# The first stage of a sparse graph kernel: other buffers, another order of row work and searches, weights loaded at its end

## The chip, the cores and the metric

The kernel runs on one core of one Trainium2 chip. The metric is the device time of one execution in microseconds. Over three runs it was 2909.53 (median; 2902.95 to 2912.19).

## What is computed

The input is a batch of 8 feature matrices x (2048 nodes by 128 features) and one adjacency matrix (2048 by 2048, 0 or 1, on average 16 ones in a row). Four graph layers follow each other:

```python
# layers 0 and 1: attention over the neighbours, 8 heads
scores = where(adj == 0, -inf, Q @ K.T / 4);  attn_out = softmax(scores) @ V
x = layer_norm(h + attn_out @ Wo + bo);  x = layer_norm(x + relu(x @ W1 + b1) @ W2 + b2)
# layers 2 and 3: graph attention
e = leaky_relu(s_i + s_j), -inf where adj == 0
x = layer_norm(softmax(e) @ (x @ W) + x)
```

## The kernel before, in words

Because the matrix is sparse, `sparse_path` (L90) never forms the 2048 by 2048 scores. For each node it makes a list of neighbours, and in each layer it gathers the neighbours' rows from a table in DRAM (keys and values of all 8 batches, 8 KB a node in layers 0 and 1). Nodes are sorted by their number of neighbours, so that 16 blocks of 128 nodes have lists of nearly equal length. A block is 128 nodes everywhere below, t counts blocks.

`start()` (L934) is the first stage. It does three things for each of 16 blocks:

- **Search.** `neighbours(t)` (L1019), on DVE: one masking pass over 128 rows of adjacency (L1022: column number where the entry isn't 0), then 16 maximum searches over segments of 128 columns (L1028), which leave 128 candidates a node. `load_adj` (L959) brings the 1 MB of adjacency over SP's queue into one of six buffers; the load for t+6 is issued when the mask of t is done. POOL stores the candidates to `found` (L1030). ACT counts the empty candidates (L1031, into `none`) and, in an iteration later, sums the kept ones (`rest`).
- **Count.** `count(t)` (L1038), on POOL for the first 15 blocks and on DVE for the last: from `none` it makes two 64-column masks, which PE adds into `places` in PSUM (L1001). After the last block, `places` gives every node its rank.
- **Rows.** `turn_x(t)` (L970): PE transposes 8 tiles of x, two ACT copies take them from PSUM, and ACT issues the load of x for block t+4. `first_rows(t)` (L978): 16 products with the key and value weights of layer 0 (L539), four ACT copies (L545) into one of two 1 MB buffers `tops`, and an ACT-issued store to the table in DRAM (L985). Block t uses the buffer of block t-2.

The loop (L1068) runs search t, count t-1, rest t-1, turning of block t-1 and rows of block t-2, in this order; each engine has its own in-order queue, so the order of these calls is the order on every engine. After the loop come the last count, turning of block 15, rows of block 14, the ranks (L1084 to L1121, which end in `perm`, the sorted order), the rows of block 15, the list of neighbours of the first block (`find_lists(0)`, L366), two DVE memsets (L1129, L1130), and `fetch()` (L1131), which issues the first ten gathers on POOL (L321). Then the rank column is copied to DRAM (L1132) and the zero rows of two tables are written (L1135).

The weights, 19 small loads in the list `waiting`, are issued on SP after the first six adjacency loads (L1064). `prepare()` (L256) readies them as a generator that is advanced at t = 4 and t = 6 of the loop, and run to its end in `layers()` (L1269): it centres columns and rows on DVE, multiplies small vectors on PE (L266, L279) into the PSUM tile `pair`, and adds the results on DVE.

The seven large buffers `bufs` hold all of this in the first stage (x in 0, turned x in 1, `tops` in 2, adjacency in 3 to 5, masks and candidates in 6) and the gathered rows afterwards, so parts that were never written are set to zero (L942, L1074, L1129, L1130).

A DMA is issued by SP, ACT or POOL. Those of SP and ACT take eight completion semaphores in turn; the compiled program lists for each DMA which earlier one its issuing engine waits for.

Of the kernel before, what the change touches and what calls it, by code (L numbers as in the profile page):

```python
# [9 lines left out]
F32 = mybir.dt.float32  # L10
# [3 lines left out]
I32 = mybir.dt.int32  # L14
AF = mybir.ActivationFunctionType
# [3 lines left out]
P = 128  # L19
# [14 lines left out]
RING = 9  # L34
STATES = 4
SCALED = 1

# [15 lines left out]
BINS = 64  # L53
# [36 lines left out]
def sparse_path(ctx: ExitStack, tc: tile.TileContext, ins: dict, out: bass.AP, flag: bass.AP):  # L90
# [157 lines left out]
    def centered(w):  # L248

        m = small.tile([P, 1], F32, tag="mean", name="mean")  # L250
        m = m[: w.shape[0], :]
        nc.vector.tensor_reduce(m, w, axis=AX.X, op=ALU.add)
        nc.vector.tensor_scalar_mul(m, m, -1.0 / D)
        nc.vector.tensor_scalar_add(w, w, m)

    def prepare():  # L256

        for l in (0, 1):
            w = W[l]
# [4 lines left out]
            pb = pair  # L264
            for f in range(2):
                nc.tensor.matmul(  # L266
                    pb[:, f : f + 1], w["1"][:, f * P : (f + 1) * P], w["col"][:, 6:7],
                    start=f == 0, stop=f == 1, skip_group_check=True,
                )
            yield  # L270
            nc.vector.tensor_sub(w["col"][:, 4:6], w["col"][:, 4:6], pb[:, :2])
            nc.vector.tensor_add(w["col"][:, 1:2], w["col"][:, 1:2], w["col"][:, 6:7])
            for f in range(2):
                centered(w["2"][:, f, :])
            yield
        for l in (2, 3):
            w = W[l]
            pa = pair
            nc.tensor.matmul(pa[:, :2], w["T"], w["col"][:, 2:4], start=True, stop=True)  # L279
            yield  # L280
            nc.vector.tensor_copy(w["h"][:, D : D + 2], pa[:, :2])
            centered(w["h"][:, :D])

    def width(l):
        return NB * (2 * D if l < 2 else D + 2)
# [246 lines left out]
    def project(l, i, xT, rows, t):  # L532

        w = W[l]
        wide = 2 * D if l < 2 else D + 2
        for h in range(i, i + 4, 2):
            pp = misc()[:, : 2 * wide].rearrange("p (b c) -> p b c", c=wide)
            for j in range(2):
                nc.tensor.matmul(  # L539
                    pp[:, j, :], xT[:, h + j, :], w["qkv"][:, D:] if l < 2 else w["h"],  # L540
                    start=j == 0, stop=True, skip_group_check=True,
                )
            yield
            if l < 2:
                nc.scalar.copy(  # L545
                    rows[:, h * wide : (h + 2) * wide], pp.rearrange("p b c -> p (b c)")
                )
# [386 lines left out]
    def start():  # L934


        adj = [bufs[3 + i // 2][:, i % 2 * N : (i % 2 + 1) * N].bitcast(I32) for i in range(6)]
        xs = [bufs[0][:, i * B * D : (i + 1) * B * D] for i in range(4)]
        xTs = [bufs[1][:, i * B * D : (i + 1) * B * D] for i in range(4)]
        tops = [bufs[2][:, i * width(0) : (i + 1) * width(0)] for i in range(2)]  # L940
        for i in range(3):
            nc.vector.memset(bufs[i][:, 2 * N :], 0.0)  # L942
        cands = bufs[6][:, NT * BINS : NT * BINS + NT * P].rearrange("p (t s c) -> p t s c", t=NT, c=8)
        falling = small.tile([P, BINS], F16, tag="falling", name="falling", bufs=1)
# [13 lines left out]

        def load_adj(t):  # L959
            if t < NT:  # L960
                nc.sync.dma_start(adj[t % 6], ins["adj"][t * P : (t + 1) * P, :])

        def load_x(t):
            if t < NT:
# [13 lines left out]
        def first_rows(t):  # L978
            if t < 0:
                return  # L980
            xT = turned(t)
            for i in range(0, B, 4):
                for _ in project(0, i, xT, tops[t % 2], t):
                    pass
            nc.scalar.dma_start(tables[0][t * P : (t + 1) * P, :], tops[t % 2])  # L985

# [32 lines left out]
        def neighbours(t):  # L1019
            val = work.tile([P, NB, D], F32, tag="q", name="val")  # L1020
            val = val.rearrange("p s c -> p (s c)").bitcast(F16)[:, :N]
            nc.vector.scalar_tensor_tensor(  # L1022
                val, adj[t % 6], 0.0, iota1, op0=ALU.not_equal, op1=ALU.mult,
                accum_out=every_sum[:, t : t + 1],
            )
            load_adj(t + 6)
            for i in range(N // SEG):
                nc.vector.max(cands[:, t, i, :], val[:, i * SEG : (i + 1) * SEG])  # L1028
# [9 lines left out]
        def count(t):  # L1038

            eng = nc.gpsimd if t + 1 < NT else nc.vector  # L1040
            d = small.tile([P, 1], F32, tag="d", name="d")
            eng.tensor_scalar_max(d, none[:, t : t + 1], float(N // SEG * 8 - BINS + 1))
# [24 lines left out]
        rest = None  # L1067
        for t in range(NT):  # L1068
            now_rest = neighbours(t)
            if t > 0:  # L1070
                count(t - 1)
                rest()
            if t in (11, 13):
                nc.gpsimd.memset(bufs[{11: 5, 13: 3}[t]], 0.0)  # L1074
            rest = now_rest
            turn_x(t - 1)
            first_rows(t - 2)
            if t in (4, 6):
                next(weights, None)
        count(NT - 1)  # L1080
        turn_x(NT - 1)
        first_rows(NT - 2)

        picked = bufs[0][:, : NT * BINS].rearrange("p (t c) -> p t c", c=BINS)  # L1084
        nc.vector.tensor_mul(picked, places, same)
        rank = small.tile([P, NT], F32, tag="rank", name="rank", bufs=1)
        nc.vector.tensor_reduce(rank, picked, axis=AX.X, op=ALU.add)
# [1 line left out]
        nc.vector.tensor_single_scalar(largest, rank, float(P), op=ALU.is_lt)  # L1089


        up = bufs[0][:, N : N + NT * (NT + 1)].rearrange("p (t h) -> p t h", h=NT + 1)
# [8 lines left out]
        high = bufs[0][:, N + 512 : N + 512 + NT * NT].rearrange("p (t h) -> p t h", h=NT)  # L1101
# [19 lines left out]
        nc.vector.tensor_add(perm, part1, pn[:, NT : 2 * NT])  # L1121
# [7 lines left out]
        nc.vector.memset(bufs[4], 0.0)  # L1129
# [731 lines left out]
```

## Time and profile before

| what | value |
|---|---|
| median of three runs | 2909.53 us |
| profiled execution | 2798.62 us |
| its span | 2796.7 us, granted TensorE clock 0.939 |
| busy, share of the span | PE 84%, DVE 90%, ACT 49%, POOL 63% |
| DMA | 973.64 MB, mean 348 GB/s |
| adjacency loads, 16 of 1024 KB | 15.6 us from issue to landing (median) |
| table stores of the first stage, 16 of 1024 KB | 4.5 us |
| x loads, 16 of 512 KB | 9.9 us |

The first stage by stretches of the profiled execution:

| us from the start | PE busy | DVE busy | ACT busy | DMA, GB/s |
|---|---|---|---|---|
| 20 to 30 | 6.14 of 10 | 9.97 | 3.13 | 312 |
| 60 to 80 | 13.34 of 20 | 19.86 | 7.78 | 423 |
| 98 to 116 | 16.46 of 18 | 0.52 | 13.70 | 258 |
| 116 to 131 | 13.01 of 15 | 9.49 | 11.47 | 151 |
| 131 to 152 | 13.14 of 21 | 15.44 | 6.29 | 235 |

How to read the profile's rows: a row of a timeline has the start in us, the busy time in us, the engine (with a q: its queue, which issues DMAs or waits), the line of the kernel, the operation, what is written from what, the shapes and the count; in square brackets stand the idle time of the engine before it and what ended that. A row of the view of waits has who waited, for what, the us in total, the times, and the longest. A row of the chain has the start, the duration and what the end of the stage hung on.

### The profile page before, as it was taken

How to read it: one execution, taken by the hardware profiler on the slowest of the kernel's cores; microseconds unless marked ns; L12 is line 12 of the kernel's file. 1: busy time of each engine (PE TensorE's matmuls, PEld its weight loads, DVE VectorE, ACT ScalarE, POOL GpSimd, SP SyncE). 2: the span in 40 equal slices, each digit the busy share in tenths (PEclk: the TensorE clock that was granted, in tenths of full speed). 3: DMA queues.
4: the chain of work that ended last, by engine and by line, in shares of the span. 5: the costliest groups of instructions: out<-in, count | busy, mean ns of one | idle time of the engine just before them, and what ended most of it. 6: DMA issues, size and time to landing. Idle time of an engine off the chain costs nothing.

```text
span 2796.7 us, 48901 instructions
## 1 busy us (share of the span) xinstructions
PE 2345.7 (84%) x17811; PEld 2126.5 (76%) x17811; DVE 2513.7 (90%) x2467; ACT 1381.6 (49%) x5032; POOL 1755.3 (63%) x1346
## 2 busy tenths in 40 slices
PE   5866889898899998798989999997677887878885
PEld 4655788787788887688878888886567776878885
DVE  9698999999899897999999999986889997799995
ACT  3611444454455665154445556566346566355554
POOL 3367788678656454545565566562776776677772
PEclk9978999999999999999999999999789888999997
DMA  9898999999999888789999999984999998999994
GB/s 365 275 373 311 369 349 345 376 338 350 369 337 355 336 320 315 306 320 369 348 390 369 354 374 368 349 328 172 367 412 413 375 367 326 347 411 413 406 402 157
DMA packets 195426, 973.64 MB, mean 348 GB/s; under 512 B 30012, under 2 KB 31804, under 8 KB 123184
## 3 DMA queue, kind: packets, MB, share of 16 engines
q0 software_dynamic: 172080, 885.06, 82.5%
q1 hardware_dynamic: 18346, 60.00, 5.5%
q10 hardware_dynamic: 4752, 25.36, 2.7%
q8 instruction: 144, 2.36, 0.3%
q14 instruction: 104, 0.85, 0.1%
HBM read 917.09 MB, written 87.36 MB: 359 GB/s over the span
## 4 chain that ended last, share of the span: by engine, by line
PE 42%; DVE 24%; DMA 16%; issue 8%; ACT 8%; POOL 1%; ACTq 0%; POOLq 0%; DVEq 0%; SPq 0%
PE acc L335 15%; DMA kv<-table,lists 9%; DVE kv L695 8%; DVE kv L657 8%; PE pair L335 4%; PE m L793 4%; PE m L776 3%; PE m L539 3%; PE m L342 2%; DVE kv L838 2%; PE m L788 2%; PE m L593 2%; PE m L759 2%; PE m L763 2%; DMA table<-rows,perm 2%
## 5 line engine op out<-in xcount | busy, mean ns | idle before, releaser
L321 POOL DMA_INDIRECT kv<-table,lists x938 | 1282.2, 1367 | 678.0 <-PE acc L335 269.8
L335 PE MATMUL acc<-ident,kv 128*128 128x128 f32 x8048 | 1052.9, 285 | 159.6 <-DVE kv L695 87.9
L335 PEld LDWEIGHTS acc<-ident,kv 128*128 128x128 f32 x8048 | 957.6, 148 | 222.4 <-DVE kv L695 111.1
L695 DVE TENSOR_TENSOR kv<-kv,weights 128x2048 f32<-128x2048 f32 (+1 forms) x282 | 625.8, 2219 | 25.9 <-ACT weights L687 25.8
L657 DVE TENSOR_TENSOR kv<-kv,q 128x2048 f32<-128x2048 f32 (+1 forms) x280 | 618.2, 2208 | 32.0 <-DMA kv<-table,lists 26.3
L838 DVE TENSOR_TENSOR kv<-kv,pair 128x3584 f32<-128x3584 f32 (+1 forms) x150 | 530.8, 3538 | 1.0
L335 PE MATMUL pair<-ident,kv 128*128 128x128 f32 (+1 forms) x2256 | 301.3, 277 | 86.1 <-issue 72.8
L663 DVE TENSOR_TENSOR kv<-kv 128x1024 f32<-128x1024 f32 (+1 forms) x282 | 334.8, 1187 | 9.2
L335 PEld LDWEIGHTS pair<-ident,kv 128*128 128x128 f32 (+1 forms) x2256 | 257.0, 141 | 106.4 <-issue 85.1
L321 POOL DMA_INDIRECT kv<-table,sorted_lists x150 | 192.8, 1286 | 139.7 <-PE acc L335 42.9
L679 ACT ACTIVATE ring<-pair 128x128 f32<-128x128 f32 (+1 forms) x282 | 77.8, 276 | 365.0 <-PE pair L335 292.9
L502 ACT ACTIVATE n<-m,eps 128x128 f32<-128x128 f32 x512 | 181.5, 371 | 137.6 <-PE m L793 133.3
L687 ACT COPY weights<-pair 128x128 f32<-128x128 f32 (+1 forms) x282 | 73.3, 260 | 350.9 <-PE pair L683 342.7
L843 ACT ACTIVATE kv<-kv,ws 128x128 f32<-128x128 f32 x544 | 174.5, 398 | 145.0 <-DVE ws L832 136.4
L793 PE MATMUL m<-w_L,hT 128*128 128x128 f32 x1024 | 157.3, 276 | 0.0
L509 ACT ACTIVATE n<-m,rs 128x128 f32<-128x128 f32 x512 | 146.4, 376 | 0.3
L793 PEld LDWEIGHTS m<-w_L,hT 128*128 128x128 f32 x1024 | 136.1, 193 | 0.0
L776 PE MATMUL m<-n1T,w_L 128*128 128x512 f32 x256 | 132.9, 604 | 3.0 <-ACT hT L781 1.8
L723 DVE TENSOR_TENSOR o<-acc,scale 128x512 f32<-128x512 f32 x128 | 83.3, 684 | 52.0 <-ACT scale L741 27.1
L526 POOL DMA_INDIRECT table<-rows,perm x57 | 82.1, 1441 | 70.1 <-ACT own L562 18.7
L342 PE MATMUL m<-ident,n 128*128 128x128 f32 x640 | 114.9, 293 | 11.9 <-ACT n L509 5.6
L342 PEld LDWEIGHTS m<-ident,n 128*128 128x128 f32 x640 | 79.6, 145 | 51.0 <-ACT n L509 23.3
(254 smaller groups left out, 3614.2 us busy)
## 6 DMA issues: line engine op xcount, KB each, us to landing
kept<-xT SPq DMA_DIRECT2D x40, 512.0 KB, 6.7
kv<-in_adj_dram SPq DMA_DIRECT2D x16, 1024.0 KB, 15.6
table<-kv ACTq DMA_DIRECT2D x16, 1024.0 KB, 4.5
xT<-kept SPq DMA_DIRECT2D x32, 512.0 KB, 8.0
kv<-table,lists POOLq DMA_INDIRECT x938, 8.6
kv<-in_x_nodes_dram ACTq DMA_DIRECT2D x16, 512.0 KB, 9.9
kv<-table,sorted_lists POOLq DMA_INDIRECT x150, 6.9
home<-kept SPq DMA_DIRECT2D x4, 512.0 KB, 15.3
```

The costliest lines, as they stand in the source:

```text
L321: this = nc.gpsimd.indirect_dma_start(out=dst, out_offset=None, in_=tables[l][:, :] if need == NT else views[l][0], in_offset=bass.Indirec ...
L335: nc.tensor.matmul(dst, src, ident, start=start, stop=True, is_transpose=True, skip_group_check=True)
L342: nc.tensor.transpose(pt[:, j * P : (j + 1) * P], src[:, j, :], ident)
L502: nc.scalar.activation(dst[:, i, :], z[:, i, :], AF.Square, bias=eps, scale=D**-0.5, accum_out=ss[:, i : i + 1],)
L509: nc.scalar.mul(dst[:, i, :], z[:, i, :], rs[:, i : i + 1])
L657: nc.vector.tensor_mul(kk, kk, q[:, None].to_broadcast([P, ns, NB, D]))
L663: nc.vector.tensor_add(hk.rearrange("p j (c h) -> p c j h", h=NH), kj[:, :, :NH, :], kj[:, :, NH:, :])
L695: nc.vector.tensor_mul(vv, vv, w.rearrange("p (s b h) -> p (s b) h", b=NB, h=NH)[:, :, None, :] .to_broadcast([P, ns * NB, HD, NH]),)
L776: nc.tensor.matmul(ph, wt["1"][:, f * P : (f + 1) * P], n1T.rearrange("p b c -> p (b c)"), start=True, stop=True,)
L793: nc.tensor.matmul(y[:, j, :], hT[:, f, j, :], wt["2"][:, f, :], start=False, stop=f == 1, skip_group_check=True,)
L838: nc.vector.tensor_mul(hv[:, :, :nv, :], hv[:, :, :nv, :], wc[:, :, :nv, None].to_broadcast([P, ns, nv, D]))
L843: nc.scalar.mul(hv[:, i, b, :], hv[:, i, b, :], ws[:, i, b - nv : b - nv + 1])
```

## The change

Four edits, all in `start()`, `prepare()` and the first lines of `layers()`:

- Buffers: four `tops` instead of two, four adjacency buffers instead of six.
- Order in the loop: search t; then, except at t = 5, 8 and 11, turning of the next block and rows of the one before it; then count t-1, rest t-1; then `ended()` with the store of candidates and the count of empty ones. So turning starts with block 0 at t = 0. Thirteen blocks are turned in the loop; block 13 is turned after the last count, 14 after `perm`, 15 after the first list. For the last block DVE counts the empty candidates itself.
- Weights: their 19 loads follow the adjacency loads on SP; the zero rows follow them, then the rank column. `prepare()` has three parts, all run in `layers()`.
- Zeroing: on POOL after `perm`, instead of POOL in the loop and DVE before the first gathers. The rank arithmetic uses buffers 3 and 6 instead of 0.

```diff
+BEHIND = (5, 8, 11)
...
-        adj = [bufs[3 + i // 2][:, i % 2 * N : (i % 2 + 1) * N].bitcast(I32) for i in range(6)]
+        adj = [bufs[3 + i // 2][:, i % 2 * N : (i % 2 + 1) * N].bitcast(I32) for i in range(4)]
...
-        tops = [bufs[2][:, i * width(0) : (i + 1) * width(0)] for i in range(2)]
-        for i in range(3):
+        tops = [bufs[2 + 3 * (i // 2)][:, i % 2 * width(0) : (i % 2 + 1) * width(0)] for i in range(4)]
+        for i in (0, 1, 2, 5):
             nc.vector.memset(bufs[i][:, 2 * N :], 0.0)
...
-            nc.gpsimd.dma_start(found[t * P : (t + 1) * P, :], every)
-            total(every, AF.Relu, none[:, t : t + 1], bias=onesc, scale=-1.0)
-            return lambda: total(every, AF.Copy, kept_sum[:, t : t + 1])
+
+            def ended():
+                nc.gpsimd.dma_start(found[t * P : (t + 1) * P, :], every)
+                if t + 1 < NT:
+                    total(every, AF.Relu, none[:, t : t + 1], bias=onesc, scale=-1.0)
+                    return
+                empty = small.tile([P, P], F32, tag="partial", name="empty")
+                nc.vector.tensor_single_scalar(empty, every, 0.0, op=ALU.is_equal)
+                nc.vector.tensor_reduce(none[:, t : t + 1], empty, axis=AX.X, op=ALU.add)
+
+            return ended, lambda: total(every, AF.Copy, kept_sum[:, t : t + 1])
...
-        for t in range(6):
+        for t in range(4):
             load_adj(t)
-            if t < 4:
-                load_x(t)
-        for dst, src in waiting:
-            nc.sync.dma_start(dst, src)
-
+            load_x(t)
         rest = None
+        turned_so_far = 0
         for t in range(NT):
-            now_rest = neighbours(t)
+            ended, now_rest = neighbours(t)
+            if t not in BEHIND:
+                turn_x(turned_so_far)
+                first_rows(turned_so_far - 1)
+                turned_so_far += 1
             if t > 0:
                 count(t - 1)
                 rest()
-            if t in (11, 13):
-                nc.gpsimd.memset(bufs[{11: 5, 13: 3}[t]], 0.0)
+            ended()
             rest = now_rest
-            turn_x(t - 1)
-            first_rows(t - 2)
-            if t in (4, 6):
-                next(weights, None)
         count(NT - 1)
-        turn_x(NT - 1)
-        first_rows(NT - 2)
+        turn_x(turned_so_far)
+        first_rows(turned_so_far - 1)
...
-        first_rows(NT - 1)
+        nc.gpsimd.memset(bufs[3], 0.0)
+        nc.gpsimd.memset(bufs[4], 0.0)
+        nc.gpsimd.memset(spot, 0.0)
+        turn_x(turned_so_far + 1)
+        first_rows(turned_so_far)
...
-        nc.vector.memset(bufs[4], 0.0)
-        nc.vector.memset(bufs[6][:, NT * (BINS + P) :], 0.0)
+        for t in range(turned_so_far + 2, NT + 1):
+            if t < NT:
+                turn_x(t)
+            first_rows(t - 1)
+        for dst, src in waiting:
+            nc.sync.dma_start(dst, src)
+        for l in (2, 3):
+            nc.sync.dma_start(tables[l][N : N + 1, :], bufs[3][:1, : width(l)])
         fetch()
         nc.sync.dma_start(ranks.rearrange("(t p) o -> p (t o)", p=P), rank)
         rest()
-        for l in (2, 3):
-            nc.sync.dma_start(tables[l][N : N + 1, :], bufs[5][:1, : width(l)])
...
         begin(every[0])
+        next(weights, None)
         drain()
```

`prepare()` after the change: the first part centres the rows and matrices of layers 0 and 1 on DVE, the second runs all small products of the four layers on PE into columns of `pair`, the third adds and copies their results on DVE.

More of the change, by code (lines that the diff above doesn't have):

```diff
@@ L263, in prepare @@
             w["row_z"] = parts(row_z, f"z{l}")
-            pb = pair
+            for f in range(2):
+                centered(w["2"][:, f, :])
+        yield
+        for l in range(4):
+            w = W[l]
+            if l > 1:
+                nc.tensor.matmul(
+                    pair[:, 2 * l : 2 * l + 2], w["T"], w["col"][:, 2:4], start=False, stop=l == 3,
+                    skip_group_check=True,
+                )
+                continue
             for f in range(2):
                 nc.tensor.matmul(
-                    pb[:, f : f + 1], w["1"][:, f * P : (f + 1) * P], w["col"][:, 6:7],
-                    start=f == 0, stop=f == 1, skip_group_check=True,
-                )
-            yield
-            nc.vector.tensor_sub(w["col"][:, 4:6], w["col"][:, 4:6], pb[:, :2])
+                    pair[:, 2 * l + f : 2 * l + f + 1], w["1"][:, f * P : (f + 1) * P],
+                    w["col"][:, 6:7], start=l + f == 0, stop=False, skip_group_check=True,
+                )
+        yield
+        for l in (0, 1):
+            w = W[l]
+            nc.vector.tensor_sub(w["col"][:, 4:6], w["col"][:, 4:6], pair[:, 2 * l : 2 * l + 2])
             nc.vector.tensor_add(w["col"][:, 1:2], w["col"][:, 1:2], w["col"][:, 6:7])
-            for f in range(2):
-                centered(w["2"][:, f, :])
-            yield
         for l in (2, 3):
[L277 to L282, printed above, removed]
+            nc.vector.tensor_copy(W[l]["h"][:, D : D + 2], pair[:, 2 * l : 2 * l + 2])
+            centered(W[l]["h"][:, :D])
     def width(l):
@@ L960, in load_adj @@
             if t < NT:
-                nc.sync.dma_start(adj[t % 6], ins["adj"][t * P : (t + 1) * P, :])
+                nc.sync.dma_start(adj[t % 4], ins["adj"][t * P : (t + 1) * P, :])
         def load_x(t):
@@ L982, in first_rows @@
             for i in range(0, B, 4):
-                for _ in project(0, i, xT, tops[t % 2], t):
+                for _ in project(0, i, xT, tops[t % 4], t):
                     pass
-            nc.scalar.dma_start(tables[0][t * P : (t + 1) * P, :], tops[t % 2])
+            nc.scalar.dma_start(tables[0][t * P : (t + 1) * P, :], tops[t % 4])
         none = small.tile([P, NT], F32, tag="none", name="none", bufs=1)
@@ L1022, in neighbours @@
             nc.vector.scalar_tensor_tensor(
-                val, adj[t % 6], 0.0, iota1, op0=ALU.not_equal, op1=ALU.mult,
+                val, adj[t % 4], 0.0, iota1, op0=ALU.not_equal, op1=ALU.mult,
                 accum_out=every_sum[:, t : t + 1],
             )
-            load_adj(t + 6)
+            load_adj(t + 4)
             for i in range(N // SEG):
@@ L1040, in count @@
             eng = nc.gpsimd if t + 1 < NT else nc.vector
-            d = small.tile([P, 1], F32, tag="d", name="d")
+            d = small.tile([P, 1], F32, tag="d" if t + 1 < NT else "mean", name="d")
             eng.tensor_scalar_max(d, none[:, t : t + 1], float(N // SEG * 8 - BINS + 1))
@@ L1072, in start @@
                 rest()
-            if t in (11, 13):
-                nc.gpsimd.memset(bufs[{11: 5, 13: 3}[t]], 0.0)
+            ended()
             rest = now_rest
-            turn_x(t - 1)
-            first_rows(t - 2)
-            if t in (4, 6):
-                next(weights, None)
         count(NT - 1)
-        turn_x(NT - 1)
-        first_rows(NT - 2)
-        picked = bufs[0][:, : NT * BINS].rearrange("p (t c) -> p t c", c=BINS)
+        turn_x(turned_so_far)
+        first_rows(turned_so_far - 1)
+        picked = bufs[3][:, : NT * BINS].rearrange("p (t c) -> p t c", c=BINS)
         nc.vector.tensor_mul(picked, places, same)
@@ L1089, in start @@
         nc.vector.tensor_single_scalar(largest, rank, float(P), op=ALU.is_lt)
-        up = bufs[0][:, N : N + NT * (NT + 1)].rearrange("p (t h) -> p t h", h=NT + 1)
+        spot = bufs[6][:, NT * (BINS + P) :]
+        up = spot[:, : NT * (NT + 1)].rearrange("p (t h) -> p t h", h=NT + 1)
         nc.vector.tensor_tensor(
@@ L1100, in start @@
         nc.vector.tensor_scalar_add(lo1, lo1, float(P + 1))
-        high = bufs[0][:, N + 512 : N + 512 + NT * NT].rearrange("p (t h) -> p t h", h=NT)
+        high = spot[:, NT * (NT + 1) : NT * (2 * NT + 1)].rearrange("p (t h) -> p t h", h=NT)
         nc.vector.tensor_sub(high, up[:, :, :NT], up[:, :, 1:])
```

## The prediction

> **What bounds the kernel now.** I read the page first: DVE is busy 90% of the span, PE 84%, and nothing in the change touches the four layers, so only the first stage, up to the first gathered rows, is in question. The view of waits, taken over the first 152 us, has one large entry on DVE and one on ACT:
>
> ```profile
> DVE d L1042 <- ACT junk L1017: 17.4, 1, 17.4
> ACT kv L545 <- DMA table<-kv: 19.9, 5, 4.3
> ACT junk L1017 <- DMA w_L<-in_L_w_dram: 3.2, 1, 3.2
> ```
>
> The timeline of DVE gives them a place:
>
> ```profile
> 92.85 2.27 DVE L1022 SCALAR_TENSOR_TENSOR val<-kv,iota 128x2048 f16<-128x2048 int32 x1
> 95.17 3.19 DVE L1028 MAX8 kv<-val 128x8 f32<-128x128 f16 x16
> 115.81 0.15 DVE L1042 TENSOR_SCALAR d<-none 128x1 f32<-128x1 f32 x1 [17.44 <-ACT junk L1017]
> 119.93 1.22 DVE L1085 TENSOR_TENSOR kv<-places,kv 128x1024 f32<-128x1024 f32 x1 [3.55 <-PE places L1001]
> ...
> 130.71 0.17 DVE L1121 TENSOR_TENSOR perm<-part,m 128x16 int32<-128x16 f32 x1
> ...
> 151.75 2.29 DVE L657 TENSOR_TENSOR kv<-kv,q 128x2048 f32<-128x2048 f32 x1 [2.14 <-DMA kv<-table,lists]
> ```
>
> The searches end at 98.36; DVE then stands until ACT has counted the last block's empty places at 115.8, because that count is queued in ACT behind the row work (turning x, projecting, storing a block). The row work goes on to the end of the stage:
>
> ```profile
> 88.84 0.33 ACTq L985 DMA_DIRECT2D table<-kv  x1
> ...
> 124.82 0.33 ACTq L985 DMA_DIRECT2D table<-kv  x1
> 125.19 4.85 ACT L1111 ACTIVATE chosen<-kv,largest 128x128 f16<-128x128 f32 x16 [0.40 <-DVE low L1113]
> ...
> 137.24 0.33 ACTq L985 DMA_DIRECT2D table<-kv  x1
> ```
>
> and the first gather on POOL stands after it:
>
> ```profile
> 142.41 1.02 POOL L321 DMA_INDIRECT kv<-table,lists  x1 [10.15 <-DVE kv L1129]
> ```
>
> A gather may read any row, so it needs all sixteen table stores. 137.24 plus the median landing of a store in the page (4.5) is 141.7; the DVE memset (L1129, ends 141.99) is named as releaser, but takes less than 1 us more. So the stage's end is the sixteenth store. What held the row work back, before it ran at 5.20 us a block (83.64 to 120.03, seven blocks), the chain of the first 160 us shows:
>
> ```profile
> 33.50 11.25 DMA table<-kv
> 44.81 22.41 DMA kv<-in_adj_dram
> 67.30 13.84 DMA table<-kv
> ```
>
> An adjacency load (44.81, landing 67.2) releases the issue of a *table store* (67.30). They share no data. In the compiled program the DMAs that SP and ACT issue take eight completion semaphores in turn, so each waits, in its issuing engine's queue, for an earlier DMA of either engine. The 3.2 us entry above is another such wait: ACT held by a weight load at its x load.
>
> **The change, part by part.** Times are on the profiled execution: 2798.62, of which 2796.7 is the span and 1.9 lies around it. It is 110.9 us (3.8%) under the median of 2909.53; I carry the difference in us over unscaled, since 3.8% of a few us is nothing.
>
> *Searches.* One is 5.43 us (92.85 less 49.42, over eight). Weight preparation leaves DVE's middle: 33.47 to 37.02 and 47.89 to 49.42, 5.1 us. From 6.31 the sixteen end at 93.2 instead of 98.36. With four adjacency buffers the load of t+4 is issued when the mask of t is done; it has 4 x 5.43 - 2.3 = 19.4 us against a median landing of 15.6 (min 5.6, max 23.4, under three or four loads in flight). Here about one is in flight, so I take 7, and no starving of DVE.
>
> *The last count on DVE*: two small operations (near 0.3 each, as L252's 0.27) in place of the 17.4 us wait. What is late next is `places`: PE does the last count's additions after the row work queued before it.
>
> *Row work first, and four table buffers.* PE starts turning x near 8 instead of 20.8, and the 19.9 us of waits for table buffers go. DMA bandwidth can carry it: by the end of the searches 16.8 MB adjacency, 8.4 MB x, 12.6 MB of tables and 0.9 MB found, 38.7 MB. From 60 to 80 us the stretches show 423 GB/s: 91.5 us. The Trainium skill (DMA: Bandwidth & Descriptors, "Where 436 GB/s comes from") says that HBM binds such transfers at about 358 GB/s: 108 us, and the searches would starve. The trace decides; I use 423.
>
> *Weights last: the new wait.* SP issues the 19 weight loads only after adjacency load 15. The compiled order names who waits for whom: table store 6 waits for adjacency load 14; the x load of block 12, issued by ACT in iteration 10, waits for L1's qkv weights, which wait for adjacency load 15; table store 7 waits for L2's column weights, seven issues further on. Load 14 cannot be issued before 6.31 + 10 x 5.43 + 2.3 = 62.9, load 15 not before 68.3. So store 6, due at 60.4, goes at about 70; load 15 lands at 75.3; qkv lands 3.5 later (its row in the page of DMAs) at 78.8, where ACT, freed by store 6 at 70 and through with turning by 72, gets on. Its four row copies take 2.7; L2's columns are issued at 75.3 + 7 x 0.45 = 78.5 and land at 82. Store 7 goes at 82, against 88.84 now. Behind the waiting DMA in ACT stand the copies that empty PSUM (so PE stops), and the counts that POOL and PE wait for.
>
> *From there to the sixteenth store.* Now: 88.84 to 137.24, 48.4. After: to store 8, 5.2 plus 2.6 for the late count of block 10 (ACT 0.7, then POOL's 1.3 + 0.46 + part of 0.44) that PE meets ahead of its next block: 89.8. Three blocks at 5.2: store 11 at 105.4. `places` 1 us later, so DVE's L1085 at 106.5 (13.4 earlier than 119.93), `perm` at 117.5. But three blocks (BEHIND skips three iterations) now come after `perm`: turning 14 (1.5) and projecting 13 as block 15 now (130.36 on PE to 137.24: 6.9): store 13 at 125.4; one turn and block at 6.5, between 5.2 and 8.4 by PE's clock (0.74 in 131 to 152): 131.9; one block without a turn, 4 to 6.9: 137. The sixteenth store is issued at 137.0, against 137.24. What the searches give is spent in the wait for weights and on the blocks behind them.
>
> *Rest.* The two memsets of DVE and the two of POOL become three on POOL, 3.56 + 3.56 + 1.0 (bounds 0.9 to 1.1), after `perm`: done at 127, hidden behind the row work by 16 us, else up to 8. All preparation (12.4 us: 5.1 from the searches, 6.5 from 143 to 149.6, 0.8 more) stands between the lists (near 127.6) and the first rows (near 153); the rows are awaited anyway; uncovered it would cost 12. The rank copy, 4-byte pieces, goes out behind weights and zero rows at 123.8, 13.2 us before the last store (now 122.44, 14.8 before). The store behind it now took 13.0 to land, not 4.5: cost 0 to 8.5; I take the shift of 1.6, as the distance is nearly that of now. Passing the 19 weights, it waits for none that is still out. First gather: 137.0 + 4.5 + 0.4 + 1.6 = 143.5, against 142.41: +1.1. The first rows follow 9.3 later, as now. Bounds: -5 (all landings at their shortest, PE's clock full) to +8.
>
> **The rivals.** *Waits do not bind* (25%): had the loads landed early enough to hold ACT nowhere, rows keep pace with the searches: store 11 at 93.2, `places` 95.5, `perm` 106.5, last store 126, gather 131.4: -11, 2898.5. For: the 17.4 and 19.9 us do go. Against: load 15 cannot be issued before 68.3, whatever lands fast.
> *ACT waits longer for weights* (30%): with the median landing of 15.6, load 15 lands at 83.9, and the columns, 7.9 after their issue as L0's w2 did, at 95. Store 7 goes 9 to 13 later, everything after it too: +10.5, 2920. It decides from store 7 at about 90 (over 0.3%). For: loads took up to 23.4. Against: those queued three deep.
> *As reckoned* (45%, own range 2903 to 2918): the gain is taken back by the order of DMAs, and the stage ends where it did.
>
> **How the numbers follow.** 2798.62 + 1.1 is 2799.7, on the median 2910.6: 2911. A measurement of this kernel can tell about 0.3%, 8.7 us, from no change. Most of the first rival lies below 2900.8, most of the second above 2918.2: 0.22 faster, 0.28 slower, 0.50 the same. Range 2895 to 2923.
>
> **What would show it.** Right: DVE's 17.4 us wait gone, searches ending near 93; ACT idle some 9 us up to 70 and 7 up to 79, named after DMAs; L1085 near 106; the sixteenth store near 137, the first gather near 143. Wrong: no such idle stretch in ACT and `places` at 96 (first rival); store 7 after 90 or DVE waiting for adjacency (second). A first product (L657) more than 12 us behind the first gather would say that the preparation is not covered.

## The result, and the profile after

The changed kernel takes 2912.73 us (median of 22 runs) against 2912.73 for the kernel before on the same chip (22 runs): ratio 1.0002, 95% interval 0.9987 to 1.0016. A second comparison on another chip, told below, gave 1.0028 (1.0013 to 1.0042). The forecast was 2911, and no change to be told.

The profiled execution of the changed kernel has a span of 2910.8 us at a mean granted clock of 0.92, that of the kernel before 2796.7 at 0.939. These 4% are not the change: the kernel before, profiled once more on another chip, had a span of 2898.3. The stretches of the two profiles of that one kernel show where two executions differ. Columns: stretch, length, busy time and count of PE, PEld, DVE, ACT and POOL, granted clock, DMA share, GB/s. First the kernel before in the profile on record:

```profile
1000.00:1800.00 800.00, 723.35 (x5614) 647.93 (x5613) 748.85 (x446) 395.99 (x1471) 445.61 (x270) 0.97 0.91 348
...
2400.00:2600.00 200.00, 161.64 (x1370) 155.98 (x1369) 176.55 (x212) 85.29 (x326) 148.45 (x148) 0.97 1.01 403
```

and the same kernel in the second profile:

```profile
1000.00:1800.00 800.00, 720.52 (x5592) 644.53 (x5591) 746.54 (x444) 396.03 (x1471) 442.10 (x268) 0.97 0.91 347
...
2400.00:2600.00 200.00, 148.91 (x1062) 137.47 (x1061) 132.76 (x151) 73.82 (x286) 115.33 (x115) 0.81 0.90 331
```

Up to 1800 us they are alike; in the last layers the clock (0.97 against 0.81) and the DMA rate (403 against 331) part. So the profiles are compared over the first stage, the first 160 us, and in one place below, on one chip, up to the end of layer 1.

The view of waits of the changed kernel, over its first 155 us (engine and line that waited, for whom: us, times, longest):

```profile
POOL kv L327 <- DMA table<-kv: 16.7, 1, 16.7
DVE kv L1095 <- PE places L1007: 16.1, 1, 16.1
...
ACT kv L551 <- DMA kv<-in_x_nodes_dram: 7.3, 2, 5.9
...
ACT kv L551 <- DMA w_L<-in_L_qkv_dram: 6.4, 1, 6.4
ACT junk L1023 <- DMA kv<-in_adj_dram: 5.8, 1, 5.8
...
DVE val L1028 <- DMA kv<-in_adj_dram: 2.8, 1, 2.8
```

DVE's 17.4 us for the late count has become 16.1 us for `places`, that is, for the row work queued on PE in front of the last count. ACT's 19.9 us for table buffers are gone; in their place it waits for loads of x, a weight load and an adjacency load, and POOL's first gather now waits 16.7 us for the table. The timeline of DVE:

```profile
90.80 3.19 DVE L1034 MAX8 kv<-val 128x8 f32<-128x128 f16 x16
...
111.36 1.23 DVE L1095 TENSOR_TENSOR kv<-places,kv 128x1024 f32<-128x1024 f32 x1 [16.09 <-PE places L1007]
122.21 0.17 DVE L1132 TENSOR_TENSOR perm<-part,m 128x16 int32<-128x16 f32 x1
...
157.19 2.29 DVE L663 TENSOR_TENSOR kv<-kv,q 128x2048 f32<-128x2048 f32 x1 [11.62 <-DMA kv<-table,lists]
```

`places` come 8.6 us earlier than before and `perm` 8.5, yet the first product of gathered rows (L657 before, L663 now) comes 5.4 us later. ACT's timeline holds the wait for the adjacency load and that for the weight load, each behind the DMA named as releaser:

```profile
72.92 0.33 ACTq L991 DMA_DIRECT2D table<-kv  x1
73.30 0.31 ACT L1023 ACTIVATE junk<-kv 128x128 f32<-128x128 f32 x1 [5.79 <-DMA kv<-in_adj_dram]
...
81.43 1.56 ACT L551 COPY kv<-m 128x512 f32<-128x512 f32 x3 [6.39 <-DMA w_L<-in_L_qkv_dram]
...
85.53 0.33 ACTq L991 DMA_DIRECT2D table<-kv  x1
...
137.14 0.42 ACTq L991 DMA_DIRECT2D table<-kv  x1
```

and POOL's has the gather that ends the stage:

```profile
148.47 1.02 POOL L327 DMA_INDIRECT kv<-table,lists  x1 [16.71 <-DMA table<-kv]
```

The sixteenth store (L991) is issued at 137.14, as before (137.24). The gather that follows it is 6.1 us later than before. That difference lies between the issue of the last store and the gather that waits for its landing.

### The profile page after: what moved, and what is told of

It is laid out like the page before. It is cut to its first block, busy times and chain, and to the rows that moved or that the text cites. A ratio compares the mean times of both kernels' runs of the same rounds, so it can differ in the third digit from the quotient of the medians.

```text
span 2910.8 us, 48909 instructions
## 1 busy us (share of the span) xinstructions
PE 2388.6 (82%) x17811; PEld 2147.2 (74%) x17811; DVE 2514.1 (86%) x2468; ACT 1380.8 (47%) x5030; POOL 1753.2 (60%) x1347
## 5 line engine op out<-in xcount | busy, mean ns | idle before, releaser
L341 PE MATMUL acc<-ident,kv 128*128 128x128 f32 x8048 | 1079.6, 286 | 208.7 <-DVE kv L701 90.4
L663 DVE TENSOR_TENSOR kv<-kv,q 128x2048 f32<-128x2048 f32 (+1 forms) x280 | 618.0, 2207 | 37.8 <-DMA kv<-table,lists 30.7
L855 DVE TENSOR_TENSOR kv<-kv 128x1024 f32<-128x1024 f32 x75 | 91.6, 1221 | 64.0 <-ACT kv L849 60.2
L348 PE MATMUL m<-ident,n 128*128 128x128 f32 x640 | 115.9, 296 | 22.6 <-ACT n L898 8.4
L890 ACT ACTIVATE ends<-m,eps 128x128 f32<-128x128 f32 x128 | 45.3, 371 | 184.3 <-PE m L882 80.9
```

Of the source, the lines that this page charges most:

```text
L341: nc.tensor.matmul(dst, src, ident, start=start, stop=True, is_transpose=True, skip_group_check=True)
L348: nc.tensor.transpose(pt[:, j * P : (j + 1) * P], src[:, j, :], ident)
L663: nc.vector.tensor_mul(kk, kk, q[:, None].to_broadcast([P, ns, NB, D]))
```

## The experiments

Theory after this result: the order of DMAs takes back what the searches gave (weights and adjacency loads hold ACT, three blocks stand behind the searches), and the rank copy lying in front of the last stores makes the stage end late. Rivals: the stores landed late for another reason; the DMA engines are full anyway, so the waits named after weights only stand for bandwidth; the skipped blocks pay.

All twelve runs, with the times of their own profiles: DVE's `places` row, issue of the sixteenth store (store 15, counted from 0), first gather, first product of gathered rows, and the ratio to the kernel before on the same chip. The comparisons were made in four groups: after (median of before 2912.73); r to r, w0, n (2790.94); n to r, w8, n, early zeroing (2910.39); and the last four rows (2901.99). "r" is the rank copy first, "w0" weights from POOL's queue at the start, "w8" from turn 8 on, "n" no block behind the searches.

| kernel | places | store 15 | gather | product | ratio (95%) |
|---|---|---|---|---|---|
| before | 119.93 | 137.24 | 142.41 | 151.75 | |
| after | 111.36 | 137.14 | 148.47 | 157.19 | 1.0002 (0.9987–1.0016) |
| r | 112.22 | 136.78 | 142.85 | 151.73 | 1.0006 (0.9994–1.0018) |
| w0 | 110.61 | 135.21 | 147.69 | 156.79 | 1.0042 (1.0027–1.0056) |
| r, w0 | 110.17 | 136.39 | 142.06 | 151.37 | 1.0014 (1.0005–1.0023) |
| r, w0, n | 110.98 | 115.00 | 131.84 | 142.93 | 0.9990 (0.9982–0.9998) |
| n | 121.40 | 125.41 | 142.16 | 155.79 | 1.0007 (0.9993–1.0020) |
| w8 | 104.22 | 130.17 | 141.93 | 150.93 | 1.0017 (1.0003–1.0032) |
| r, w8, n | 107.78 | 111.79 | 128.67 | 140.75 | 0.9995 (0.9980–1.0010) |
| r, w8, n, early zeroing | 107.70 | 111.72 | 126.20 | 146.01 | 0.9997 (0.9982–1.0011) |
| before, again | 119.43 | 139.13 | 144.54 | 153.71 | one run |
| after, again | 113.42 | 138.99 | 151.41 | 160.97 | 1.0028 (1.0013–1.0042) |
| before, gather put off | 119.54 | 138.10 | 153.81 | 163.01 | 1.0028 (1.0012–1.0045) |
| r, w0, n, again | 112.46 | 116.47 | 133.32 | 146.66 | 0.9999 (0.9983–1.0015) |

The kernel before itself moved its first product by 2.0 us between its two profiles, so a difference of that size between rows says nothing.

### The rank copy first

```diff
+        nc.sync.dma_start(ranks.rearrange("(t p) o -> p (t o)", p=P), rank)
         for l in (2, 3):
             nc.sync.dma_start(tables[l][N : N + 1, :], bufs[3][:1, : width(l)])
         fetch()
-        nc.sync.dma_start(ranks.rearrange("(t p) o -> p (t o)", p=P), rank)
```

> One edit to the changed kernel: the copy of the ranks to DRAM is issued ahead of the zero rows of tables 2 and 3 on SP's queue, so it goes out when the rank is there (about 114 us) and not at 127.98. My theory (the copy's four-byte pieces hold up store 15 of the table): the copy is over before store 15, which still goes out near 137 and lands about 4.5 us later instead of 11.3; first gather near 142 (148.5 in the changed kernel), first product of gathered rows near 151.5 (157.2), so some 6 us off the total, 0.998 of the changed kernel. Rival (the slow landing has another cause, the zero rows or the memsets beside it): first gather stays near 148 and the time does not move.

The gather came at 142.85 and the product at 151.73, as the theory had it; the store was issued where it was (136.78). The DMA view shows where the time goes: GB/s in 40 slices of 1 us, from 110 to 150 us. The kernel before, which issues the copy at 122.44:

```profile
GB/s 254 369 393 33 8 164 451 426 8 0 123 401 393 134 13 123 49 16 57 49 16 16 25 16 106 303 299 393 455 418 279 16 0 0 147 336 418 344 385 402
```

The changed kernel:

```profile
GB/s 53 131 393 385 156 0 0 393 442 213 0 0 0 0 90 283 152 0 9 7 132 49 25 49 57 8 33 25 106 426 434 418 401 418 451 107 25 0 0 0
...
q1 hardware_dynamic: 2068, 0.02, 2.3%
```

and with the rank copy first:

```profile
GB/s 66 16 147 459 410 51 6 57 123 33 33 8 82 41 66 74 197 369 373 316 451 410 0 0 393 393 262 221 410 393 33 8 0 0 106 197 401 385 377 393
```

q1 holds SP's transfers: 2048 four-byte pieces of the rank column and a few others, 0.02 MB in all. In the changed kernel it is issued at 127.98, and from slice 19 (128 to 129) to slice 28 hardly anything moves, though stores 13, 14 and 15 are issued at 129.17, 133.68 and 137.14. Then what is left of all three, most of 3 MB, passes together, at 400 to 450 GB/s until 145 and the rest by 147; the gather follows at 148.47. With the copy issued at 114.73 the empty stretch lies from 115 to 126: store 12 (issued at 117.11) landed 11.8 us after its issue, the copy itself after 12.2, stores 13 and 14 after 3.9 each. So the stretch moves with the copy: for some ten us after its issue 1 MB stores of another engine's queue hardly get on, and what counts is how many of those ten us the last store has left to wait. That is shown. The trace's records of single packets say a little of how: in the changed kernel the copy's pieces all start between 128.2 and 130.3, 7 ns each, and from 130.1 on the stores' packets of 8 KB do start, but take 2.8 us each (median of 49, up to 138.5), against 0.31 from 139 on. As far as these records tell, then, the stores do not stand in line behind the pieces; their own packets are slow. What slows them, no run here shows. On the whole kernel the 5.5 us by which the first product came earlier cannot be told: 1.0006 beside 1.0002 and 1.0028 for the changed kernel.

### The weights on POOL's queue

```diff
+        for dst, src in waiting:
+            nc.gpsimd.dma_start(dst, src)
         rest = None
...
-        for dst, src in waiting:
-            nc.sync.dma_start(dst, src)
```

> One edit to the changed kernel: the sixteen weight loads are issued from GpSimd's queue, ahead of the loop over blocks, so no load of x waits for a weight. My theory (ScalarE is held up 6.4 + 1.1 us by the weights): those waits are gone, store 7 of the table goes out near 77 instead of 85.5, store 15 near 129 instead of 137.1; the rank copy is then issued near 119 and still lies in front of the last store, so that the first gather is near 140 and the first product near 149 (157.2): 8 us off the total. Rival (the adjacency loads and the rate of the DMA engines hold ScalarE anyway): store 7 stays at 84 or later, and the time does not move.

> Both edits to the changed kernel: ranks copied ahead of the zero rows, and weights loaded from GpSimd's queue. My theory: store 15 near 129, landing 4.5 us later, first gather near 133.5, first product near 142.5 (157.2 in the changed kernel, 151.75 in the kernel before): some 9 us, or 0.997 of the kernel before. Rival: one of the two waits is replaced by the lists or by GpSimd's memsets, and the first product is at 149 or later.

Neither came out (the list has 19 loads, not sixteen). The 6.4 and 1.1 us waits did go, but the start is slower: PE waits 8.9 us for the first loads of x, not 6.8, and POOL issues weights until 23.9, so that PE waits another 3.3 us for POOL's first masks. The third table store went at 39.0, not at 31.1, and store 7 at 83.0. Most of what was won at the weights was lost in front of them. With the rank copy moved as well, store 15 was issued at 136.39 (129 expected) and the product came at 151.37 (142.5 expected). Store 7 at 83.0 lies next to the rival's 84, but w0 cannot tell the two apart, because it also moves the load in time, so it was done again with the weights from turn 8 on:

```diff
             ended()
+            for dst, src in waiting[4 * (t - 8) : 4 * (t - 7)] if t >= 8 else ():
+                nc.gpsimd.dma_start(dst, src)
...
-        for dst, src in waiting:
-            nc.sync.dma_start(dst, src)
```

> One edit to the changed kernel: the weight loads go out from GpSimd's queue in the turns of blocks 8 to 12, four at a time, so they neither share completion semaphores with the loads of x nor take the DMA engines at the start. My theory (ScalarE lost 6.4 + 1.1 us to the weights' semaphores): store 0 stays near 21, the two waits are gone, store 7 near 78, places near 104, store 15 near 130, first product near 150 (157.2), the rank copy still in the way. Rival (the DMA engines are full up to 85 us, so the loads of x come no earlier): store 7 stays at 84 or later and places at 110 or later.

This one did: store 0 at 20.48, store 7 at 74.93 (78 expected, 85.53 in the changed kernel), `places` at 104.22, store 15 at 130.17, product at 150.93. The waits for weights were waits for a completion semaphore and not for bandwidth: with the same bytes from a queue with other semaphores, at the same part of the stage (issued from 63.9 to 88.7), no wait of ACT for a weight is left, and `places` came 7.1 us earlier. In the changed kernel the DMA engines moved 305 GB/s while ACT waited (72 to 84 us), in w8 413 (72 to 82). The edit also took away the wait in front of store 6 (67.95, not 72.92). The trace has the semaphore of each DMA: there are eight for SP and ACT, and store 6 shares its one with adjacency load 14 (issued at 63.66) in the changed kernel, but with load 12 (52.34) in w8, where no weights stand between in the turn. The loads were not free: POOL spends about 0.55 us on issuing each, and in the skipped turn four stand in front of masks that PE needs:

```profile
80.13 0.21 PE L1007 MATMUL places<-kv,earlier 128*128 128x64 bf16 x1 [4.55 <-POOL kv L1057]
```

The gather still waited for the rank copy, issued at 120.90, 1.3 us ahead of store 13.

### No block behind the searches

```diff
-BEHIND = (5, 8, 11)
+BEHIND = ()
...
-            if t < 0:
+            if t < 0 or t >= NT:
```

The second edit, made in `turn_x` and `first_rows`, only keeps the call after the loop from turning a block 16.

> As the last, and in addition no block's features are put behind the searches: the features of every block are made in the block's own turn. My theory (skipped turns at the start put the stores back by the time ScalarE has nothing else): places near 100 (111.4 in the changed kernel), permutation near 111, first gather near 121, first product near 130, 22 us ahead of the kernel before: 0.9925. Rival: with the features in their old place VectorE starves again as in the kernel before (searches end near 106 and not 94), and the first product is no earlier than 142.

> One edit to the changed kernel: no features are put behind the searches (BEHIND is empty), weights and ranks stay where the change has them. My theory, from the run without skipped turns: in a skipped turn TensorE stands at the count of a block that VectorE is still searching, ScalarE has nothing for some 4 us, and the three blocks of features (about 4.5 us each) come after the choice of the large nodes instead; so places about where they were (111 to 116 us), but store 15 near 118 and not 137, ahead of the rank copy, first gather near 134 behind the lists, first product near 146 (157.2 in the changed kernel, 151.75 in the kernel before): 0.998 of the kernel before. Rival (the skipped turns do bring places forward, as they were meant to): places come at 122 or later, the permutation at 132, first product at 154 or later, and nothing is won.

> Three edits to the changed kernel: weights from GpSimd's queue in the turns of blocks 8 to 12, ranks copied ahead of the zero rows, no features behind the searches. My theory: ScalarE's turns of 5.2 us follow the searches closely; store 15 near 106, places near 102, permutation near 112, lists near 122, first gather near 123 and first product near 134: 18 us ahead of the kernel before, 0.994. Rival (the rate of the DMA engines sets when x arrives, whoever asks): places at 109 or later and first product at 141 or later, as in the run with the weights loaded at the start.

Alone it brought `places` at 121.40 and the product at 155.79: theory and rival each half right. Row work without skips reaches the late loads sooner and waits longer; the view of waits, first 155 us, of this kernel:

```profile
ACT kv L551 <- DMA kv<-in_adj_dram: 7.0, 1, 7.0
...
ACT junk L1023 <- DMA w_L_col<-in_L_col_dram: 6.1, 1, 6.1
```

Between stores 6 (63.52) and 7 (81.71) lie 18.2 us. The first gather, 142.16, then follows POOL's memsets (done at 141.1). So with the weights on SP, the skips do bring `places` forward, by 10.0 us, and put store 15 back, by 11.7. Take the weights out of the way, and little speaks for them: from w8 to r, w8, n (the rank copy is moved too) `places` are 3.6 us later and store 15 is 18.4 us earlier. What a skipped turn costs shows in PE's timeline of the changed kernel:

```profile
87.62 0.21 PE L1007 MATMUL places<-kv,earlier 128*128 128x64 bf16 x1 [3.38 <-POOL kv L1057]
88.31 0.21 PE L1007 MATMUL places<-sofar,ones_bf 128*128 128x64 bf16 x1 [0.47 <-POOL sofar L1067]
88.41 1.94 PE L348 MATMUL m<-ident,kv 128*128 128x128 f32 x8
...
99.82 1.07 PE L348 MATMUL m<-ident,kv 128*128 128x128 f32 x8
```

PE works in the order of the calls. In the skipped turn it has only the count of block 10. Its masks come from POOL (86.8 to 87.6), which waits for ACT's count of empty places (86.2), which stands behind store 7; so PE waits 3.4 us, and the next block's turning (L348) stands behind. In the other turns the row work lies in front of the count and covers that way. After the gap the turning takes 1.94 us, at a granted clock of 0.72 (88.4 to 95 us), against 1.07 at 1.00 (95 to 111). And the block itself is still to be done after `perm`.

The searches did not starve in r, w0, n: they ended at 93.7 (that rival gives 106 for the kernel before, whose searches ended at 98.36). With rank copy and weights out of the way and no skips, the first product comes at 142.93 and 140.75. Expected were 130 and 134: store 15 no longer ends the stage there (111.79), and the lists do; then the preparation, which I had costed at nothing because the rows are awaited anyway, is late next. The timeline of DVE in r, w8, n:

```profile
123.50 4.14 DVE L417 TENSOR_SCALAR lmask<-top 128x29 bf16<-128x29 f32 x1
...
127.69 0.19 DVE L423 SCALAR_TENSOR_TENSOR lists<-top,far 128x29 int32<-128x29 f32 x1
127.79 0.28 DVE L253 TENSOR_REDUCE mean<-w_L 128x1 f32<-128x128 f32 x1
...
140.44 0.29 DVE L255 TENSOR_SCALAR w_L_h<-w_L_h,mean 128x128 f32<-128x128 f32 x1
140.75 2.29 DVE L663 TENSOR_TENSOR kv<-kv,q 128x2048 f32<-128x2048 f32 x1
```

From 127.79 DVE prepares weights with one pause of 0.75 us, and the first product follows it at once, with no wait for rows.

### The zeroing early

```diff
+        nc.gpsimd.memset(bufs[4], 0.0)
+        nc.gpsimd.memset(bufs[3][:, NT * BINS :], 0.0)
         picked = bufs[3][:, : NT * BINS].rearrange("p (t c) -> p t c", c=BINS)
...
-        nc.gpsimd.memset(bufs[3], 0.0)
-        nc.gpsimd.memset(bufs[4], 0.0)
+        nc.gpsimd.memset(bufs[3][:, : NT * BINS], 0.0)
```

> As the last, and in addition GpSimd's zeroing of the two buffers of gathered rows is done as soon as the searches end (only 1024 columns of one of them wait until the ranks are out). My theory (in the changed kernel the two rows of the lists took 2.7 us each beside GpSimd's memsets, where 0.2 is their length otherwise, and the first gather stands behind 8 us of memsets): lists 2 to 4 us earlier than in the last run, first gather and first product as much earlier, 0.001 of the total. Rival (GpSimd's memsets do not hold VectorE): lists and first product where they were.

The first half held. The same operation, in DVE's timeline of this kernel, beside 4.14 us above:

```profile
124.92 0.18 DVE L417 TENSOR_SCALAR lmask<-top 128x29 bf16<-128x29 f32 x1
...
144.08 0.16 DVE L284 TENSOR_TENSOR w_L_col<-w_L_col,pair 128x2 f32<-128x2 f32 x1 [8.53 <-remote]
...
146.01 2.29 DVE L663 TENSOR_TENSOR kv<-kv,q 128x2048 f32<-128x2048 f32 x1
```

A DVE operation of 0.18 us lasted 4.14 beside POOL's memsets. In r, w8, n it began at 123.50, inside a memset of 3.59 us, and ended at 127.64, 0.05 after the next memset (1.03 us) had ended; in the changed kernel it took 2.71 and ended at 131.80, 0.03 after the last memset there. The Trainium skill (SBUF — State Buffer, "SBUF: two separate sides") says that GpSimd and VectorE, in some forms of VectorE's operations, share a port pair under a lock held for a whole instruction, and that the loser stands; these times agree, and here the loser stood until both memsets were done. But the gather, 2.5 us earlier (126.20), did not bring the product earlier: the third part of the preparation waited 8.5 us for something that the profile gives only as "remote", and the product stands behind it. That stays open.

### Does a shift of the stage reach the end?

```diff
         advance(threads)
+        for _ in range(6):
+            nc.gpsimd.memset(bufs[4], 0.0)
...
-        nc.vector.memset(bufs[4], 0.0)
```

> The kernel before, unchanged, with a profile taken on the same chip as the next three, since the profiled executions compared so far stand 4% apart in their last 900 us. First product of gathered rows at 151.7 as in the profile on record; where the first-stage difference to the changed kernel goes is to be read from the times of the same gathers in this and the next profile.

> The kernel before with its first gather put off: GpSimd zeroes one buffer six times (3.56 us each, 21 us from 131.5) instead of VectorE once, so the first gather is near 153.5 and not 142.4 and the first product near 163, 11 us later; nothing else is changed. If a shift of the first product is carried to the end one for one: 1.0038 of the kernel before. If it is taken up on the way: within 1.0010.

> The changed kernel, unchanged, on the same chip. First product near 157.2, 5.4 us after the kernel before. If a shift of the first product is carried to the end one for one, the time is 1.002 of the kernel before; if it is taken up on the way, 1.000, and the gathers of the two profiles meet within the first layers.

> The version with weights from GpSimd's queue at the start, ranks copied first and no features behind the searches, once more on this chip: first product near 142.9, 8.8 us ahead of the kernel before. Carried one for one 0.997; taken up on the way 1.000; the run on another chip gave 0.9990.

These four runs, the last rows of the table, were made on one chip. The kernel before with its first product 9.3 us later (163.01 against 153.71) lost 0.28%, 8.1 us (interval 3.5 to 13). The changed kernel, 7.3 us later on this chip, lost as much (3.8 to 12.2). The version without skips, 7.0 us ahead, gained nothing (0.9999; on the other chip 8.8 us ahead of the profile of before on record, 0.9990).

That looks like delays carried to the end one for one, and for the put-off gather it may be so. For the other two the profiles of this chip show something else. The last product of gathered rows in layer 1, first in the kernel before, then in the changed kernel:

```profile
1879.07 2.29 DVE L657 TENSOR_TENSOR kv<-kv,q 128x2048 f32<-128x2048 f32 x1
```

```profile
1878.25 2.28 DVE L663 TENSOR_TENSOR kv<-kv,q 128x2048 f32<-128x2048 f32 x1
```

and in the version without skips:

```profile
1864.76 2.28 DVE L663 TENSOR_TENSOR kv<-kv,q 128x2048 f32<-128x2048 f32 x1
```

With the put-off gather it is at 1885.10. So by the end of layer 1 the changed kernel has made up its 7.3 us and is 0.8 ahead. Most of that is made up early, where DVE waits for gathered rows: the fifteenth product is at 246.50 in the kernel before, after a wait of 5.7 us, and at 249.01 in the changed kernel, after 2.4. The put-off gather is still 6.0 late, and the lead without skips has grown from 7.0 to 14.3. What the changed kernel lost in the total, and the lead of 14.3, went in layers 2 and 3. Why is open. These are single profiles, and from there on two of one kernel differ by up to 100 us; and every changed version that was run beside the kernel before has a lower mean granted clock than it (by 0.002 to 0.007), which may be cause or effect.

A line through the twelve ratios, each times its median of before, against the shift of the first product has a slope of 0.5, a scatter of 3 us and 3 us at no shift. (In the second and third group the shift is taken against the profile on record.) So a first stage that ends earlier or later is a poor measure of the total: half of a shift is seen there, with intervals of 4 us.

The first run of the version without skips was faster than before by 0.10% (0.02 to 0.18), the second by nothing (−0.15 to 0.17): no version here beats the kernel before by an amount that shows twice.

## Why the prediction was right, and where it was not

*The gain taken back by the order of DMAs: shown.* The searches ended at 93.99 (93.2 reckoned), and DVE never starved between them: its one wait for adjacency, 2.8 us, is that for the very first load, which let the first mask begin at 7.05 and not at 6.31. The wait of ACT at store 6 was 5.8 us up to 72.9 (9 up to 70 reckoned), that at the x load of block 12 was 6.4 up to 81.0 (7 up to 78.8), and store 7 went at 85.53 (82). The names of the awaited DMAs, an adjacency load and L1's qkv, were the ones read from the compiled order, and w8 shows that it was the semaphores and not the bytes. (ACT also waited 7.3 us for loads of x between 41 and 55 us, which the forecast did not have; store 6's own wait came after it.)

*From there to the sixteenth store: right at its end by luck, as two errors cancel.* Store 7 to store 8 took 9.85 us and not 7.8. The late count was about as reckoned (PE's turning starts 2.9 us after store 7, 2.6 reckoned), but the block behind it took 7.0 from turning to store and not 5.2: 6.0 is usual (99.82 to 105.78), since turning starts ahead of the store before, and the slower clock after the gap added 1.0. Stores 8 to 11 took 15.6 as reckoned. So `places` came at 111.36 (106.5) and `perm` at 122.21 (117.5). But the three blocks behind it were shorter: from `perm` to store 13 took 7.0 us (7.9 reckoned), from there to store 15 took 8.0 (11.6). Result 137.14 (137.0).

*The step that failed inside the range is the rank copy, in "cost 0 to 8.5; I take the shift of 1.6, as the distance is nearly that of now".* The copy was issued at 127.98, 9.2 us ahead of the last store, and not at 123.8, 13.2 ahead. It stands on SP behind the zero rows, which read the buffer that POOL zeroes after `perm`; `perm` was 4.7 us late, so the copy was, while the last store was not. And "nearly that of now" was the wrong way to weigh it: the profile of before showed one store landing 13.0 us after its issue, ten of them a stretch in which hardly anything moves, so that a last store inside the stretch pays what is left of it, and then queues with the stores held before it. With the gather at 148.47 in place of 137.14 + 4.5 + 0.4 = 142.0, the term measured 6.4. r takes 5.6 of it away. The total still fell inside, since 5 us are 0.17%. And the 5 us did not last: at the end of layer 1 this profile is no later than that of the kernel before (1874.49, before 1876.09). The forecast carried its first-stage shift to the end unchanged, which only the put-off gather bears out.

*Right*: the memsets (done at 131.8) and the preparation (done at 145.6) were hidden in the changed kernel; the rows followed the gather by 8.7 us (9.3). Their covers are thin, as r, w8, n showed: without the wait for the table the preparation is on the path.

*The rivals.* "Waits do not bind" would have been 11 us faster; even r, w8, n, without the waits for weights and with the rank copy out of the way, gained 1.4 us (−2.9 to 5.8) in the total, with its first product 11.0 us ahead. "ACT waits longer for weights" did not happen at its threshold: store 7 went at 85.5, not after 90. The second comparison (1.0028) lies near the forecast's upper end of "the same"; both together, 1.0015, are 4.4 us.

## What to carry to other kernels

An issue waits, in the order of its engine, for a semaphore used eight DMAs ago, whoever issued that one: when loads are put late on one queue, list in the compiled order which issues of the other queue they share semaphores with, and what stands behind those. A copy in four-byte pieces is costed by the time in which hardly anything else moves (some ten us here), and its place is where no awaited transfer falls into that time. When a stage's end is cleared, look at once for what was hidden under it: here lists, memsets and preparation were each within some ten us of becoming the end. And follow a lead of the first stage through the layers before counting on it: here one of 7 us was 14 at the end of layer 1 and nothing in the total.

## What the hardware showed that was not expected

- After the issue of a copy of 8 KB in 2048 pieces on SP's queue, three 1 MB stores on ACT's queue hardly moved until ten us had passed: 7 to 132 GB/s in all, and 400 to 450 afterwards. The Trainium skill (DMA: Bandwidth & Descriptors, "Rules for kernel authors") says that a non-contiguous last dimension becomes one descriptor per element; q1's 2068 packets agree. It says in the same place that the queues share the engines and interleave. The trace does not contradict that, as the stores' packets started when the last pieces did, but they took 2.8 us instead of 0.31, which that rule does not lead one to expect.
- From 40 to 70 us the changed kernel moved 421 GB/s, near the 423 that the forecast took from the trace of the kernel before.
- One kernel differed by 3.6% in span between two profiles (2796.7 and 2898.3), nearly all of it after 1800 us; from 2400 to 2600 us the granted clock was 0.97 in one and 0.81 in the other. Its medians on three chips were 2790.94, 2901.99 and 2910.39.
